# Applying a layer normalisation on ScalarE with scale and shift instead of on VectorE

## The chip, the core and the metric

The kernel runs on one core of a Trainium2 chip. The metric is the device time of one execution in microseconds, the median of three runs. Before the change it is 1572.69 us (1570.96 to 1573.69). The profile is of one further execution (1568.4 us, a traced span of 1566.6 us).

## What is computed

The input x has 32 graphs of 512 nodes with 128 features, and adj is a 512 by 512 adjacency. Layer 0 is a graph convolution with powers one to three of adj, layer 1 a gated graph network of five steps. Both add their input and normalise each node over its 128 features, with no learned gain:

```
m = mean(x);  v = var(x);  norm(x) = (x - m) / sqrt(v + 1e-5)
x = norm(x + conv(x, adj, weight_1))
h = x
five times:
    a  = adj @ h;  u3 = h @ u3_w.T + u3_b
    z  = sigmoid([a, a] @ w3_w.T + w3_b + u3)
    r  = sigmoid([a, a] @ w4_w.T + w4_b + u3)
    hv = tanh([a, a] @ w5_w.T + w5_b + (r * h) @ u5_w.T + u5_b)
    h  = (1 - z) * h + z * hv
out = norm(x + h)
```

## The kernel before

**Tiling.** The graphs are taken in 16 pairs (`pair(q)`, L584). Of each graph, 128 partitions hold nodes, with four groups of 128 features in the free dimension; the gates work on the transposed form (`hT`, features on partitions, 512 nodes). A product of adj by the state is made from seven block products instead of eight (`adj_product`, L349): sums S of blocks of the state are made on GpSimd (L372), TensorE multiplies them (L377), ScalarE copies partial sums out of PSUM into Q (L402, L412, L415), and VectorE adds (L404, L416, L422). Each next block product into the same PSUM bank waits for the copy of the one before it.

**One step of the gates** (`gates`, L545): TensorE multiplies by w4, w3, w5 and u5 (L550); VectorE adds biases (L555, L562), ScalarE applies sigmoids and tanh (L557, L564, L566, L576), VectorE makes `rh` (L558), GpSimd `rest` = (1 - z) * h (L569), and VectorE the new state hT (L578, L580). Then hT is brought back to nodes on partitions as X: for pairs below 15 by VectorE's 32 by 32 transposes (L333), a write to DRAM in four parts (L325) and a read back (L331); in pair 15 by TensorE (L251) and a copy (L632).

**The norms.** `norm` (L287) is used twice a pair and layer. In layer 0 it reads v, the copy of the convolution's result out of PSUM (L514), and writes `h0`; after the last step it reads and writes y, the sum of X and h0 (L643, GpSimd). For four groups of 128 features it takes moments on VectorE (L295, L296), then on GpSimd 1/sqrt(v + eps) for all four at once (`power`, L299 add and L300 power), then four applies on VectorE: (x - mean) * rstd (L303).

**The order.** Nothing is scheduled by hand. `Plan` (L41) records each operation with its engine, a planned duration, the operations that it follows, buffers that it takes and gives back, and a key. `run` (L69) plays a list schedule with these durations: each engine, when free, takes the ready operation with the smallest key. The instructions are written out in the order in which this play issues them, and each engine then works through its list in that order, whatever the real durations are. Keys grow by 33 from pair to pair and by 20 from step to step, so several pairs are in work at once, two at a time in the steps.

Of the kernel before, what the change touches and what calls it, by code (L numbers as in the profile page):

```python
# [9 lines left out]
F32 = mybir.dt.float32  # L10
AF = mybir.ActivationFunctionType
ALU = mybir.AluOpType
PSUM = bass.MemoryType.PSUM

P = 128
# [105 lines left out]
def gnn_resnorm_kernel(  # L121
# [17 lines left out]
    nc = tc.nc  # L139
# [147 lines left out]
    def norm(n, name, src_of, dst_of, after, give, key):  # L287

        mv = small.tile([P, n, 2], F32, tag="mv", name=f"mv_{name}")
        rstd = small.tile([P, n], F32, tag="rstd", name=f"rstd_{name}")  # L290
        got = []

        def moments(i):
            st = small.tile([P, 6], F32, tag="st", name=f"st_{name}_{i}")
            nc.vector.bn_stats(st, src_of(i))  # L295
            nc.vector.bn_aggr(mv[:, i, :], st)  # L296

        def power():
            nc.gpsimd.tensor_scalar(rstd, mv[:, :, 1], EPS, None, ALU.add)  # L299
            nc.gpsimd.tensor_tensor(rstd, rstd, mhalf[:, :n], ALU.pow)  # L300

        def apply(i):
            nc.vector.tensor_scalar(  # L303
                dst_of(i), src_of(i), mv[:, i, 0:1], rstd[:, i : i + 1], ALU.subtract, ALU.mult
            )

        for i in range(n):
            got.append(plan("DVE", 0.43, lambda i=i: moments(i), after=after, key=key))
        p = plan("POOL", 1.25, power, after=got, key=key)
        over = []  # L310
        for i in range(n):
            last = i == n - 1
            over.append(
                plan("DVE", 0.29, lambda i=i: apply(i), after=[p] + over, give=give if last else [], key=key)
            )
        return over

    def turn(src_of, dst_of, name, after, key, take=()):

        def put():
            for g in range(NR):
                nc.sync.dma_start(  # L325
                    plan[f"d{name}"][:, :, g, :].rearrange("r l f -> l r f"),
                    plan[f"v{name}"][g * R : (g + 1) * R, :].rearrange("l (r f) -> l r f", r=NR),
                )

        def fetch():  # L330
            nc.sync.dma_start(dst_of(), plan[f"d{name}"].rearrange("r l g f -> (r l) (g f)"))  # L331

        blocks = lambda: nc.vector.transpose(plan[f"v{name}"], src_of())  # L333
        t = plan("DVE", 0.75, blocks, after=after, take=[("v", f"v{name}")], key=key)
        t = plan("SP", 1.76, put, after=[t], take=[("d", f"d{name}")], give=[("v", f"v{name}")], key=key, late=1.8)
        return plan("SP", 0.35, fetch, after=[t], give=[("d", f"d{name}")], take=take, key=key, late=2.8)

# [11 lines left out]
    def adj_product(X_of, turned, name, m, after, key):  # L349
# [12 lines left out]
        def copied(i, block, after, take=()):  # L362

            on_act = i < 6
            to = nc.scalar.copy if on_act else nc.gpsimd.tensor_copy
            emit = lambda: to(fitted(i), block())  # L366
            engine, us = ("ACT", 0.4) if on_act else ("POOL", 0.75)
            return plan(engine, us, emit, after=after, take=take, key=key)

        def add(i, a, b, op):  # L370
# [13 lines left out]
                )  # L384

        def pool(i, a, b, op, after, take=()):
            return plan("POOL", 0.8, lambda: add(i, a, b, op), after=after, take=take, key=key)

        def pe(bank, left, right, first, last, after, take=(), give=()):
            emit = lambda: product(bank, left, right, first, last)  # L390
# [154 lines left out]
    def gates(q, s, b, name, m, h, h_new, after, u_done, key):  # L545

        mT, uT = m[1], f"uT{name}"
        pr, pz, ph = (f"b{g}{name}" for g in "rzh")
        rh, z, rest = (f"{g}{name}" for g in ("rh", "z", "rest"))
        mm = lambda dst, w, src, first, last: nc.tensor.matmul(  # L550
            plan[dst], lhsT=w, rhs=plan[src], start=first, stop=last
        )
        take = [("bank", pr), ("rh", rh), ("z", z), ("rest", rest), ("hT", h_new)]
        p = plan("PE", 0.86, lambda: mm(pr, w4s, mT, True, True), after=after + weights, take=take, key=key)
        emit = lambda: nc.vector.scalar_tensor_tensor(plan[pr], plan[pr], b4s, plan[uT], ALU.add, ALU.add)  # L555
        r = plan("DVE", 0.75, emit, after=[p, u_done], key=key)
        r = plan("ACT", 0.59, lambda: nc.scalar.activation(plan[pr], plan[pr], AF.Sigmoid), after=[r], key=key)  # L557
        emit = lambda: nc.vector.tensor_tensor(plan[rh], plan[pr], plan[h], ALU.mult)  # L558
        r = plan("DVE", 0.69, emit, after=[r], give=[("bank", pr)], key=key)

        p2 = plan("PE", 0.86, lambda: mm(pz, w3s, mT, True, True), after=[p], take=[("bank", pz)], key=key + 0.5)
        emit = lambda: nc.vector.scalar_tensor_tensor(plan[pz], plan[pz], b3s, plan[uT], ALU.add, ALU.add)  # L562
        t = plan("DVE", 0.75, emit, after=[p2, u_done], give=[("uT", uT)], key=key + 0.5)
        emit = lambda: nc.scalar.activation(plan[z], plan[pz], AF.Sigmoid)  # L564
        zs = plan("ACT", 0.59, emit, after=[t], key=key + 0.5)
        emit = lambda: nc.scalar.activation(plan[rest], plan[pz], AF.Sigmoid, scale=-1.0)  # L566
        t = plan("ACT", 0.59, emit, after=[t, zs], give=[("bank", pz)], key=key + 0.5)

        emit = lambda: nc.gpsimd.tensor_tensor(plan[rest], plan[rest], plan[h], ALU.mult)  # L569
        keep = plan("POOL", 1.3, emit, after=[t], key=key + 0.5)  # L570

        p3 = plan(
            "PE", 0.86, lambda: mm(ph, w5s, mT, True, False), after=[p2], take=[("bank", ph)], give=[m], key=key + 0.7
        )
        p4 = plan("PE", 0.86, lambda: mm(ph, u5s, rh, False, True), after=[p3, r], give=[("rh", rh)], key=key + 0.8)
        emit = lambda: nc.scalar.activation(plan[ph], plan[ph], AF.Tanh, bias=hv_b)  # L576
        t = plan("ACT", 0.66, emit, after=[p4], key=key + 0.8)
        emit = lambda: nc.vector.tensor_tensor(plan[ph], plan[ph], plan[z], ALU.mult)  # L578
        t = plan("DVE", 0.69, emit, after=[t, zs], give=[("z", z)], key=key + 0.8)
        emit = lambda: nc.vector.tensor_tensor(plan[h_new], plan[ph], plan[rest], ALU.add)  # L580
        give = [("bank", ph), ("rest", rest), ("hT", h)]
        return plan("DVE", 0.69, emit, after=[t, keep], give=give, key=key + 0.8)

    def pair(q):  # L584
# [6 lines left out]
        for s in range(STEPS):  # L591
# [25 lines left out]
            for b in range(2):  # L617
                nm = f"{name}_{b}"
                h_new = f"hT{nm}"
                g = gates(q, s, b, nm, m[b], h[b], h_new, got[b], u_done[b], key + 10)  # L620
                h[b] = h_new
                h_done.append([g])
                X_b = lambda b=b, name=name: plan[f"X{name}"][:, b]
                if q < TURNED:
                    h_of = lambda h_new=h_new: plan[h_new].rearrange("p (k r l) -> p r k l", r=NR, k=NK)
                    t = turn(h_of, X_b, nm, [g, x_slot], key + 15)
                else:
                    bn = f"bt{nm}"
                    emit = lambda bn=bn, h_new=h_new: transposes(plan[bn], lambda k: plan[h_new][:, chunk(k)])
                    t = plan("PE", 0.44, emit, after=[g, x_slot], take=[("bank", bn)], key=key + 15)  # L630

                    emit = lambda bn=bn, X_b=X_b: nc.scalar.copy(X_b(), plan[bn])  # L632
                    t = plan("ACT", 0.59, emit, after=[t], give=[("bank", bn)], key=key + 15)
                after.append([t])
                if not last:
                    continue

                i = 2 * q + b
                y = f"y{i}"

                def emit(b=b, y=y, X_new=X_new):
                    fit = lambda t: t.rearrange("p k (s d) -> p k s d", d=R) if q < TURNED else t
                    nc.gpsimd.tensor_tensor(fit(plan[y]), X_new(b), fit(plan[f"h0{q}"][:, b]), ALU.add)  # L643

                t = plan("POOL", 1.5, emit, after=[t], take=[("y", y)], key=key + 17)
                done.append(t)
                y_of = lambda k, y=y: plan[y][:, k, :]
                over = norm(NK, f"1_{i}", y_of, y_of, [t], [], key + 17)
                emit = lambda i=i, y=y: nc.sync.dma_start(out[i].rearrange("(p k) c -> p k c", k=NK), plan[y])
                plan("SP", 0.36, emit, after=over, give=[("y", y)], key=key + 17, late=2.0)  # L650
# [63 lines left out]
```

## Time and profile before

| | busy us | share of the span | instructions |
|---|---|---|---|
| TensorE (PE) | 1525.6 | 97% | 5944 |
| VectorE (DVE) | 990.3 | 63% | 2111 |
| ScalarE (ACT) | 703.9 | 45% | 1416 |
| GpSimd (POOL) | 610.7 | 39% | 770 |

| part of the norms | engine | count | mean ns |
|---|---|---|---|
| moments, L295 (layer 0 / last) | DVE | 128 / 128 | 270 / 267 |
| moments, L296 | DVE | 256 | 182 |
| add eps, L299 | POOL | 64 | 227 |
| power, L300 | POOL | 64 | 1036 |
| apply to h, L303 | DVE | 128 | 377 |
| apply to y, L303 | DVE | 128 | 582 |

Busy time is the time that an engine spends inside instructions. Moments of two kinds follow each other closely and overlap, so their lengths don't simply add. In a line of the timeline the columns are: start and length in us, engine, source line, operation, tiles written and read, and in brackets how long the engine had stood idle before it and what released it. TensorE is the busiest engine by far; the shares of the others say little before it is known in which places TensorE stands. The granted TensorE clock is 0.997 of full speed over the span.

### The profile page before, as it was taken

What the parts mean: (1) busy time and instruction counts of PE and PEld (TensorE: products, weight loads), DVE (VectorE), ACT (ScalarE), POOL (GpSimd) and SP (SyncE); (2) the same over time, 40 slices, a digit from 0 to 9 for tenths busy, and PEclk for the clock granted to TensorE, in tenths of its full rate; (3) what the DMA queues carried; (4) which work ended last, traced back from release to release, by engine and by line L of the source; (5) the groups of instructions that cost most, each with busy time, mean ns of one, the idle gap of its engine ahead of it and who ended that gap; (6) DMA issues with size and microseconds to landing.
All of it is one profiled execution on the core that took longest, in us unless ns stands there. A gap on an engine that the chain in (4) does not pass through costs nothing.

```text
span 1566.6 us, 19093 instructions
## 1 busy us (share of the span) xinstructions
PE 1525.6 (97%) x5944; PEld 1042.2 (67%) x5944; DVE 990.3 (63%) x2111; ACT 703.9 (45%) x1416; POOL 610.7 (39%) x770
## 2 busy tenths in 40 slices
PE   8999999999999999999999999999999999999995
PEld 6776676766767667676666766667676676766663
DVE  2455648576584765748666585765848657486756
ACT  2344435444353543535444444443535435356553
POOL 1233325334353352625334343343523526254434
PEclk9999999999999999999999999999999999999998
DMA  4021424224152421524323152231523223232211
GB/s 119 14 77 46 123 53 133 83 73 116 29 153 61 105 84 46 143 54 121 84 72 110 46 135 81 75 114 31 151 61 108 68 54 95 54 86 63 68 44 38
DMA packets 160181, 128.10 MB, mean 82 GB/s; under 512 B 18384, under 2 KB 124880, under 8 KB 160080
## 3 DMA queue, kind: packets, MB, share of 16 engines
q1 hardware_dynamic: 160080, 126.89, 29.9%
q8 instruction: 47, 0.77, 0.2%
q14 instruction: 54, 0.44, 0.1%
HBM read 64.42 MB, written 62.39 MB: 81 GB/s over the span
## 4 chain that ended last, share of the span: by engine, by line
PE 80%; DVE 8%; POOL 4%; DMA 2%; issue 2%; SPq 1%; ACT 1%; POOLq 0%; DVEq 0%; ACTq 0%
PE bank L550 30%; PE bank L377 28%; PE bank L598 7%; PE bank L488 7%; PE bank L499 4%; PE bank L458 3%; DVE y L303 3%; POOL y L643 2%; POOL rstd L300 1%; DMA X<-d 1%; DVE bank L555 1%; SPq L325 1%; POOL S L372 1%; PE bank L265 1%; DVE hT L580 1%
## 5 line engine op out<-in xcount | busy, mean ns | idle before, releaser
L569 POOL TENSOR_TENSOR rest<-rest,hT 128x512 f32<-128x512 f32 x160 | 203.0, 1270 | 704.5 <-ACT rest L566 704.2
L377 PE MATMUL bank<-T,S 128*128 128x256 f32 x1392 | 351.1, 380 | 1.6 <-ACT Q L412 1.5
L377 PEld LDWEIGHTS bank<-T,S 128*128 128x128 f32 x1392 | 263.0, 190 | 94.9 <-issue 25.3
L377 PE MATMUL bank<-at,S 128*128 128x256 f32 x864 | 222.1, 380 | 2.1 <-ACT S L366 1.2
L377 PEld LDWEIGHTS bank<-at,S 128*128 128x128 f32 x864 | 164.0, 190 | 51.2 <-issue 25.0
L578 DVE TENSOR_TENSOR bank<-bank,z 128x512 f32<-128x512 f32 x160 | 111.5, 697 | 120.7 <-ACT bank L576 120.6
L550 PE MATMUL bank<-m,w4s 128*128 128x512 f32 x320 | 155.7, 593 | 0.0
L550 PE MATMUL bank<-m,w3s 128*128 128x512 f32 x320 | 155.2, 593 | 0.0
L598 PE MATMUL bank<-hT,u3s 128*128 128x512 f32 x320 | 153.4, 593 | 0.0
L550 PE MATMUL bank<-rh,u5s 128*128 128x512 f32 x320 | 153.1, 593 | 0.3 <-DVE rh L558 0.3
L550 PE MATMUL bank<-m,w5s 128*128 128x512 f32 x320 | 152.7, 593 | 0.0
L372 POOL TENSOR_TENSOR S<-X 128x256 f32<-128x256 f32 x128 | 91.1, 727 | 142.3 <-DMA X<-d 141.3
L576 ACT ACTIVATE bank<-bank,hv_b 128x512 f32<-128x512 f32 x160 | 106.0, 662 | 75.2 <-PE bank L550 75.1
L557 ACT ACTIVATE bank<-bank 128x512 f32<-128x512 f32 x160 | 93.3, 583 | 99.6 <-DVE bank L555 97.2
L555 DVE SCALAR_TENSOR_TENSOR bank<-bank,b4s,uT 128x512 f32<-128x512 f32 x160 | 118.3, 746 | 30.0 <-PE bank L550 28.3
L603 ACT ACTIVATE uT<-bank,ub3s 128x512 f32<-128x512 f32 x160 | 108.8, 691 | 52.6 <-PE bank L598 50.5
L412 ACT COPY Q<-bank 128x256 f32<-128x256 f32 x96 | 36.0, 375 | 213.7 <-PE bank L377 213.6
L562 DVE SCALAR_TENSOR_TENSOR bank<-bank,b3s,uT 128x512 f32<-128x512 f32 x160 | 120.0, 751 | 2.8 <-PE bank L550 1.2
L488 PE MATMUL bank<-U,at 128*128 128x256 f32 x512 | 118.2, 380 | 0.0
L564 ACT ACTIVATE z<-bank 128x512 f32<-128x512 f32 x160 | 95.6, 597 | 43.3 <-DVE bank L562 41.7
L558 DVE TENSOR_TENSOR rh<-bank,hT 128x512 f32<-128x512 f32 x160 | 107.8, 681 | 10.3 <-ACT bank L557 10.0
L580 DVE TENSOR_TENSOR hT<-bank,rest 128x512 f32<-128x512 f32 x160 | 107.0, 676 | 4.6 <-POOL rest L569 0.2
(94 smaller groups left out, 2163.9 us busy)
## 6 DMA issues: line engine op xcount, KB each, us to landing
d<-v SPq DMA_DIRECT2D x824, 64.0 KB, 1.8
X<-d SPq DMA_DIRECT2D x150, 256.0 KB, 2.8
v<-d SPq DMA_DIRECT2D x56, 256.0 KB, 2.9
xg<-in_x SPq DMA_DIRECT2D x32, 256.0 KB, 2.9
out<-y SPq DMA_DIRECT2D x32, 256.0 KB, 2.0
at<-in_adjT SPq DMA_DIRECT2D x4, 256.0 KB, 5.3
X<-in_w SPq DMA_DIRECT2D x1, 448.0 KB, 6.2
rh<-in_w SPq DMA_DIRECT2D x3, 128.0 KB, 6.1
```

Source lines behind the costliest of these rows:

```text
L372: nc.gpsimd.tensor_tensor(fitted(i), a, b, op)
L377: nc.tensor.matmul(half(bank), lhsT=a[:, k, :], rhs=right[:, k, :], start=(first and k == 0), stop=(last and k == H - 1), skip_group_check ...
L488: nc.tensor.matmul(y_of()[:, j].rearrange("p b o -> p (b o)"), lhsT=at2[:, k, chunk(ko)], rhs=plan[f"U{q}"][:, k].rearrange("p b o -> p (b ...
L550: mm = lambda dst, w, src, first, last: nc.tensor.matmul(plan[dst], lhsT=w, rhs=plan[src], start=first, stop=last)
L555: emit = lambda: nc.vector.scalar_tensor_tensor(plan[pr], plan[pr], b4s, plan[uT], ALU.add, ALU.add)
L558: emit = lambda: nc.vector.tensor_tensor(plan[rh], plan[pr], plan[h], ALU.mult)
L562: emit = lambda: nc.vector.scalar_tensor_tensor(plan[pz], plan[pz], b3s, plan[uT], ALU.add, ALU.add)
L569: emit = lambda: nc.gpsimd.tensor_tensor(plan[rest], plan[rest], plan[h], ALU.mult)
L578: emit = lambda: nc.vector.tensor_tensor(plan[ph], plan[ph], plan[z], ALU.mult)
L580: emit = lambda: nc.vector.tensor_tensor(plan[h_new], plan[ph], plan[rest], ALU.add)
L598: emit = lambda bn=bn, hb=h[b]: nc.tensor.matmul(plan[bn], lhsT=u3s, rhs=plan[hb], start=True, stop=True)
L603: emit = lambda bn=bn, uT=uT: nc.scalar.activation(plan[uT], plan[bn], AF.Identity, bias=ub3s)
```

## The change

The apply becomes x * rstd + shift on ScalarE, with shift = -mean * rstd, which GpSimd makes in two more instructions for four groups at once. It is meant to take work off VectorE, whose queue holds the gates' additions. Beside that, planned durations are brought to what the trace shows; they only affect the order that the plan writes.

```diff
+        shift = small.tile([P, n], F32, tag="shift", name=f"shift_{name}")
...
         def power():
             nc.gpsimd.tensor_scalar(rstd, mv[:, :, 1], EPS, None, ALU.add)
+            nc.gpsimd.tensor_scalar(shift, mv[:, :, 0], -1.0, None, ALU.mult)
             nc.gpsimd.tensor_tensor(rstd, rstd, mhalf[:, :n], ALU.pow)
+            nc.gpsimd.tensor_tensor(shift, shift, rstd, ALU.mult)
 
         def apply(i):
-            nc.vector.tensor_scalar(
-                dst_of(i), src_of(i), mv[:, i, 0:1], rstd[:, i : i + 1], ALU.subtract, ALU.mult
+            nc.scalar.activation(
+                dst_of(i), src_of(i), AF.Identity, bias=shift[:, i : i + 1], scale=rstd[:, i : i + 1]
             )
 
         for i in range(n):
-            got.append(plan("DVE", 0.43, lambda i=i: moments(i), after=after, key=key))
-        p = plan("POOL", 1.25, power, after=got, key=key)
+            got.append(plan("DVE", 0.45, lambda i=i: moments(i), after=after, key=key))
+        p = plan("POOL", 1.75, power, after=got, key=key)
...
-                plan("DVE", 0.29, lambda i=i: apply(i), after=[p] + over, give=give if last else [], key=key)
+                plan("ACT", 0.3, lambda i=i: apply(i), after=[p] + over, give=give if last else [], key=key)
...
-        t = plan("DVE", 0.75, blocks, after=after, take=[("v", f"v{name}")], key=key)
+        t = plan("DVE", 0.7, blocks, after=after, take=[("v", f"v{name}")], key=key)
...
-            engine, us = ("ACT", 0.4) if on_act else ("POOL", 0.75)
+            engine, us = ("ACT", 0.41) if on_act else ("POOL", 0.4)
...
-            return plan("POOL", 0.8, lambda: add(i, a, b, op), after=after, take=take, key=key)
+            return plan("POOL", 0.73, lambda: add(i, a, b, op), after=after, take=take, key=key)
...
-        keep = plan("POOL", 1.3, emit, after=[t], key=key + 0.5)
+        keep = plan("POOL", 1.27, emit, after=[t], key=key + 0.5)
...
-                t = plan("POOL", 1.5, emit, after=[t], take=[("y", y)], key=key + 17)
+                t = plan("POOL", 1.27, emit, after=[t], take=[("y", y)], key=key + 17)
```

After the change all lines of the kernel below L303 stand three lines further down (the apply at L306, S sums at L375, Q copies at L405, L415 and L418, `rest` at L572).

## The prediction

> **What bounds the kernel now.** I read the busy table first, then the stretches of time, then what TensorE waited for.
>
> ```profile
> PE 1525.6 (97%) x5944; PEld 1042.2 (67%) x5944; DVE 990.3 (63%) x2111; ACT 703.9 (45%) x1416; POOL 610.7 (39%) x770
> ```
>
> TensorE is busy 1525.6 of 1566.6 us, and the change leaves its 5944 matmuls alone. So no edit can win more than the 41 us in which it stands. Where these lie, by stretch (the second number is TensorE's busy time):
>
> ```profile
> 0.00:40.00 40.00, 35.00 (x145) 24.80 (x146) 11.63 (x26) 8.91 (x17) 6.31 (x14) 1.00 0.40 117
> 1530.00:1540.00 10.00, 5.95 (x23) 3.05 (x22) 8.37 (x28) 5.00 (x9) 8.89 (x11) 1.00 0.07 26
> 1540.00:1550.00 10.00, 9.08 (x33) 5.77 (x32) 3.84 (x7) 2.49 (x6) 0.86 (x2) 1.00 0.07 26
> 1550.00:1567.00 17.00, 5.07 (x16) 2.27 (x14) 9.38 (x31) 4.58 (x8) 7.55 (x8) 0.67 0.08 31
> ```
>
> 5.0 us go to the first loads, 4.1 + 0.9 + 11.9 = 16.9 us to the end after 1530; about 19 us are left for the 1490 us between. TensorE's waits from 40 to 1530 us (total, times, longest) name them:
>
> ```profile
> PE bank L377 <- ACT Q L415: 15.8, 12, 1.9
> PE bank L377 <- ACT S L366: 1.2, 1, 1.2
> PE bank L377 <- ACT Q L412: 1.0, 2, 0.6
> ```
>
> Eleven of the twelve are one to a pair, from 240 to 1282 us (0.8 to 1.9 each). The timeline of one:
>
> ```profile
> 648.42 1.03 POOL L300 TENSOR_TENSOR rstd<-rstd,mhalf 128x4 f32<-128x4 f32 x1
> ...
> 649.06 3.91 DVE L303 TENSOR_SCALAR y<-y,mv,rstd 128x128 f32<-128x128 f32 x6
> ...
> 653.22 0.55 DVE L303 TENSOR_SCALAR y<-y,mv,rstd 128x128 f32<-128x128 f32 x1
> 653.69 1.40 DVE L555 SCALAR_TENSOR_TENSOR bank<-bank,b4s,uT 128x512 f32<-128x512 f32 x2
> ...
> 654.47 1.24 ACT L557 ACTIVATE bank<-bank 128x512 f32<-128x512 f32 x2 [1.74 <-DVE bank L555]
> ...
> 655.62 0.38 ACT L415 COPY Q<-bank 128x256 f32<-128x256 f32 x1
> ...
> 656.05 1.13 PE L377 MATMUL bank<-T,h 128*128 128x256 f32 x4 [1.14 <-ACT Q L415]
> ```
>
> VectorE spends 5.2 us on eight applies of the last normalisation (648.17 to 653.77), each between GpSimd's S sums; its L555 starts late; ScalarE, in order, stands in front of the sigmoid that needs L555; the copy L415 behind it comes late; TensorE stands 1.14 us. The cause is how long an apply takes (shortest, median, longest ns):
>
> ```profile
> L303 DVE TENSOR_SCALAR h<-v,mv,rstd x128: 304/340/883, 53.5 to 1377.3; 128x128 f32<-128x128 f32 x128
> L303 DVE TENSOR_SCALAR y<-y,mv,rstd x128: 297/743/883, 268.6 to 1563.2; 128x128 f32<-128x128 f32 x128
> ```
>
> The planner books 0.29 us for each. The layer-0 applies fit (0.34); the last ones take 0.74, about a GpSimd sum (0.727), so the written order is wrong just there.
>
> **What the Trainium skill says.** "SBUF — State Buffer", section "SBUF: two separate sides": VectorE and GpSimd share one port pair under an exclusive lock, and the loser "fully blocks"; ScalarE has its own ports. The trace agrees in size: 743 ns beside GpSimd against 297 alone. "VectorE: DVE Perf Modes", section "The perf-mode tier table", gives an fp32 tensor_scalar in SBUF the 2x mode, the one that needs both ports; this fits the 297 ns against 378 for a two-input 128x128 add. "ScalarE: Activation LUTs", section "Rules for kernel authors", prices an ACTIVATE with a bias pointer at about 0.3 us + 0.83 ns per element. The trace has no 128-wide one; its slope agrees ((585 - 373) ns / 256 = 0.83).
>
> **Part by part.**
>
> *Applies leave VectorE.* 256 instructions, 69.4 + 41.9 = 111.3 us, to about 879. Off the path but for the eleven places above, where eight applies booked at 2.3 us took 5.2; with them goes the cause of 15.3 us (15.8 less a last wait of 0.5 at 1470 to 1530, in the end's own stretch).
>
> *Applies come to ScalarE.* A 256-wide SBUF copy takes 410 ns; 128 elements less is -106; a bias adds 79 (tanh 662 against sigmoid 583) to 106 (L603 691 against 585). So 383 to 410 ns; the page's price gives 406. I take 400. Two L603 in a row took 1.28 us, so the second adds about 0.1 less than its length: a pitch of 0.3, which is what the plan now books. 256 x 0.4 = 102 us, ScalarE 806 us (51%). Identity is used by L603 and the trace has two table loads in all, so none is added.
>
> *Two more GpSimd instructions a norm.* A tensor_scalar of 128x4 takes 227 ns (L299). For the product, a line through 256 wide (727) and 512 wide (1270) gives 193 ns at four; I take 0.23, ends 0.19 and 0.73. With gaps as between L299 and L300 (0.08) a norm goes from 1.33 us (646.79 to 648.12) to about 1.9; planned 1.75. 64 x 0.46 = +29 us busy, GpSimd 641 us (41%). Queued behind it stand S sums (L375 after the change) and `rest` products (L572), for which TensorE and VectorE wait.
>
> *New wait on ScalarE.* The first apply waits for the shift; behind it in its queue stand copies Q, for which TensorE waits. I walked the changed program's written order at the same place, zero at the first matmul of `at` by `h`, one product or 512-wide matmul per 0.86 us. hT transposes stand earlier on VectorE, so X lands at about -5.7 and -3.8 instead of -2.2; both y sums end at -2.5, both `rest` products at 0.1, the first power at 2.0. The first S sum ends at 2.7, needed at 3.4. The second power runs 3.4 to 5.3, the next S sum ends at 6.0, needed at 6.0. ScalarE's applies end at 7.2, its copy Q is due at 7.1 and its successor product at 8.6. Nothing stands by much, but GpSimd has no slack: I leave 0.3 us a pair, 11 x 0.3 = 3.3, with 0 and 1.0 as ends. The layer-0 norm, walked likewise from 612 us, has its applies between L606 and the copies, done 0.1 us before a copy is due: 0.
>
> *Planned durations.* The changed numbers agree with the rows (0.40 for GpSimd's copy at 397 ns, 1.27 for L569, 0.73 for L372). They cost nothing; the order that follows from them is in the walks.
>
> *The end.* In pair 15 nothing fills TensorE. Now:
>
> ```profile
> 1527.33 0.68 DVE L558 TENSOR_TENSOR rh<-bank,hT 128x512 f32<-128x512 f32 x1
> ...
> 1529.48 1.26 POOL L643 TENSOR_TENSOR y<-X,h 128x512 f32<-128x512 f32 x1 [8.58 <-DMA X<-d]
> ...
> 1536.60 0.68 DVE L580 TENSOR_TENSOR hT<-bank,rest 128x512 f32<-128x512 f32 x1
> ```
>
> The changed order puts both moments of pair 14 (16 instructions, 3.1 us) ahead of both `rh`, and both powers ahead of both `rest` products. Counted from the gate's first matmul (1524.75): y ready at 2.1 to 4.7 (three products earlier than now, since pair 14's gates stand further ahead), moments end at 6.5, `rh` 7.9 (now 4.5), second power 8.8, `rest` on ScalarE between applies at 12.6, on GpSimd 14.3, second hT 15.1. Now it is 12.5 (1537.28). So +2.6. The final norm: power +0.6, four applies at a pitch of 0.3 and a last of 0.4 against 1.08: +0.2. Together +3.4.
>
> **Sum**: -15.3 + 3.3 + 3.4 = -8.6 us: 1572.7 - 8.6 = 1564.1.
>
> **The rivals.**
> - *All of it (0.15).* No stall is left, and y comes early enough that the end loses only the final norm: -15.3 + 0.8: 1558.2. For it: accurate durations. Against: the order of the end as written.
> - *GpSimd takes the stall over (0.11).* X lands 1 to 1.5 us later than I walked, and each microsecond goes through y, `rest`, power and S sum to TensorE: 11 x 1.0: -15.3 + 11 + 3.4 = -0.9: 1571.8. For it: GpSimd's longest waits are for transfers (X<-d 141 us). Against: VectorE frees hT earlier.
> - *ScalarE is blocked (0.12), slower.* An apply that waits for GpSimd holds a copy Q for about 0.9 us (half a power) in both norms of 15 pairs: 27 us, -15.3 + 27 + 3.4 = +15.1: 1587.8. For it: ScalarE's queue is in order and feeds TensorE three times a product. Against: in the trace it stands 5.6 us before L412 in just that place (5.61 at 652.36).
>
> **How the numbers follow.** The forecast (0.62) spans 1559 to 1568, since residual stalls of 0 to 0.7 a pair and an end of +0.8 to +5 both belong to it. 1556 to 1572 takes in the first two rivals and leaves out the slow one and the tails. Faster by 3.1 us or more (below 1569.5): 0.62 + 0.15 + a little of the second rival = 0.80; same 0.08; slower (above 1575.8) 0.12.
>
> **What would show it.** Right: the row PE L377 <- ACT Q (L418 after the change) falls from 15.8 to under 4 us; `rest` and hT of the last step come later from 1525 on, TensorE's idle after 1530 grows by about 3; applies near 400 ns, whichever buffer. Wrong: TensorE's waits name POOL S, or ScalarE's longest idle is an apply waiting for POOL shift with TensorE standing at once after; or applies of 0.6 us.

## The result, and the profile after

The changed kernel takes 1559.8 us (median of six runs, 1557.2 to 1562.6), the kernel before 1572.7 us in the same comparison (1569.2 to 1574.0). The ratio is 0.9922, with a 95% interval from 0.9906 to 0.9938. The forecast was 1564.1 us in a range of 1556 to 1572, so the direction and the range held, and the gain was 12.9 us instead of 8.6. The traced spans of the profiled executions are 1566.6 us before and 1555.4 us after; what follows explains these 11.2 us.

First the busy table of the changed kernel:

```profile
PE 1524.5 (98%) x5944; PEld 1041.3 (67%) x5944; DVE 894.2 (57%) x1855; ACT 801.9 (52%) x1672; POOL 635.8 (41%) x898
```

TensorE does the same work in the same busy time (1525.6 before). VectorE lost 96 us, ScalarE gained 98 and GpSimd 25. These shares are no explanation of the gain; what TensorE waited for is. From 40 to 1511 us (up to the gates of pair 15's fourth step) its waits are, in us in total, times and longest:

```profile
PE bank L380 <- POOL S L375: 2.9, 5, 1.2
PE bank L380 <- ACT Q L415: 2.4, 2, 1.9
PE bank L380 <- ACT Q L418: 0.9, 2, 0.5
```

From 240 to 1300 us only the first of these rows is left. The kernel before has this row there and no other:

```profile
PE bank L377 <- ACT Q L415: 15.3, 11, 1.9
```

The place that the prediction showed at 648 us now reads as follows (timeline after: start, length, engine, line, operation, tiles; in brackets the idle time before and what ended it):

```profile
638.78 0.23 POOL L300 TENSOR_SCALAR rstd<-mv 128x4 f32<-128x4 f32 x1
639.10 0.23 POOL L301 TENSOR_SCALAR shift<-mv 128x4 f32<-128x4 f32 x1
639.29 1.04 POOL L302 TENSOR_TENSOR rstd<-rstd,mhalf 128x4 f32<-128x4 f32 x1
...
640.40 0.20 POOL L303 TENSOR_TENSOR shift<-shift,rstd 128x4 f32<-128x4 f32 x1
...
640.55 1.42 POOL L375 TENSOR_TENSOR S<-h 128x256 f32<-128x256 f32 x2
...
640.64 1.65 ACT L306 ACTIVATE y<-y,shift,rstd 128x128 f32<-128x128 f32 x4 [0.32 <-POOL shift L303]
...
641.42 1.05 PE L380 MATMUL bank<-T,S 128*128 128x256 f32 x4
```

GpSimd needs 1.82 us for one norm (638.78 to 640.60). The four applies follow on ScalarE in 1.65 us, a pitch of 0.39, beside two S sums that no longer hold them back. No bracket stands behind the TensorE line: it did not wait.

The idle time in a row of waits understates what a stall costs. It counts from the recorded end of the matmul before, and a matmul of 256 columns is recorded with 0.38 us where the next usually starts after 0.22; that hides 0.16 us of each stall. And after each of the stalls from 240 to 1300 us the second matmul started 0.32 us behind the first instead of 0.22. So I measured the loss from start to start: each matmul's start, less the start of the one before and the usual distance of such a pair. For pair 15, where nothing fills TensorE, I took whole stretches: E is the first matmul by w4 of its fourth step, F that of its fifth.

| us | before | after | difference |
|---|---|---|---|
| lost, 40 to 240 | 3.96 | 2.49 | -1.5 |
| lost, 240 to 1300 | 18.66 | 4.67 | -14.0 |
| from E to F | 21.53 | 24.96 | +3.4 |
| from F to the end | 20.3 | 21.4 | +1.1 |
| sum | | | -11.0 |

The four rows give 11.0 of the 11.2 us by which the spans differ.

### The profile page after: what moved, and what is told of

The parts are those of the page before. It is cut to its first block, busy times and chain, and to the rows that moved or that the text cites. A ratio compares the mean times of both kernels' runs of the same rounds, so it can differ in the third digit from the quotient of the medians.

```text
span 1555.4 us, 19232 instructions
## 1 busy us (share of the span) xinstructions
PE 1524.5 (98%) x5944; PEld 1041.3 (67%) x5944; DVE 894.2 (57%) x1855; ACT 801.9 (52%) x1672; POOL 635.8 (41%) x898
## 4 chain that ended last, share of the span: by engine, by line
PE 92%; POOL 2%; issue 2%; DMA 1%; DVE 1%; ACT 1%; SPq 0%; ACTq 0%; POOLq 0%; DVEq 0%
PE bank L380 35%; PE bank L553 33%; PE bank L601 8%; PE bank L491 7%; PE bank L461 4%; PE bank L502 4%; PE bank L265 1%; DMA X<-d 1%; POOL rest L572 1%; PE bank L251 1%; POOL S L375 1%; POOL rstd L302 0%; POOL y L646 0%; SPq L328 0%; DMA at<-in_adjT 0%
## 5 line engine op out<-in xcount | busy, mean ns | idle before, releaser
L572 POOL TENSOR_TENSOR rest<-rest,hT 128x512 f32<-128x512 f32 x160 | 202.7, 1270 | 590.7 <-ACT rest L569 586.5
L375 POOL TENSOR_TENSOR S<-X 128x256 f32<-128x256 f32 x128 | 91.1, 726 | 150.0 <-DMA X<-d 132.5
L553 PEld LDWEIGHTS bank<-rh,u5s 128*128 128x128 f32 x320 | 60.7, 190 | 70.8 <-issue 58.8
```

Source lines behind the costliest of these rows:

```text
L375: nc.gpsimd.tensor_tensor(fitted(i), a, b, op)
L553: mm = lambda dst, w, src, first, last: nc.tensor.matmul(plan[dst], lhsT=w, rhs=plan[src], start=first, stop=last)
```

## The end of the changed kernel

The end gave back 4.5 us. The timeline after, around the fourth step of pair 15 (E is at 1509.05):

```profile
1514.81 1.25 DVE L561 TENSOR_TENSOR rh<-bank,hT 128x512 f32<-128x512 f32 x2
...
1515.53 1.98 PE L553 MATMUL bank<-rh,u5s 128*128 128x512 f32 x4 [1.17 <-DVE rh L561]
...
1520.16 2.49 POOL L572 TENSOR_TENSOR rest<-rest,hT 128x512 f32<-128x512 f32 x2 [3.02 <-ACT rest L569]
...
1522.20 1.11 PE L251 MATMUL bank<-ident,hT 128*128 128x128 f32 x4 [4.69 <-DVE hT L583]
1522.86 0.69 DVE L583 TENSOR_TENSOR hT<-bank,rest 128x512 f32<-128x512 f32 x1
...
1523.11 1.91 PE L601 MATMUL bank<-hT,u3s 128*128 128x512 f32 x2
...
1524.82 0.91 PE L251 MATMUL bank<-ident,hT 128*128 128x128 f32 x4
```

Both `rh` are made at E+5.8 to E+7.0, behind the sixteen moments of pair 14; before, the second ended at E+4.5. Both `rest` products are done at E+13.6. The second hT ends at 1523.55, which is E+14.5 against E+12.5 before: 2.0 us from the order. The rest is of another kind. TensorE had stood 4.69 us; the windows of the same stretch show what it then ran at (length; busy time of PE, PEld, DVE, ACT, POOL; granted clock; DMA share; GB/s):

```profile
1518.00:1522.00 4.00, 0.00 (x0) 0.00 (x0) 1.24 (x2) 3.49 (x8) 1.84 (x2) 1.00 0.28 109
1522.00:1525.00 3.00, 2.80 (x7) 1.66 (x8) 1.45 (x3) 0.59 (x1) 1.37 (x2) 0.50 0.02 8
```

At a granted clock of 0.50 the four transposes took 1.11 us and the two matmuls by u3s 1.91 us. In the kernel before, where TensorE had stood 2.13 us, it was 0.66 and 1.02 us:

```profile
1533.91 0.66 PE L251 MATMUL bank<-ident,hT 128*128 128x128 f32 x4 [2.13 <-DVE hT L580]
1534.40 1.02 PE L598 MATMUL bank<-hT,u3s 128*128 128x512 f32 x2
...
1537.34 0.66 PE L251 MATMUL bank<-ident,hT 128*128 128x128 f32 x4 [1.91 <-DVE hT L580]
```

So the second transposes start 1.3 us after their hT (1523.55 to 1524.82) instead of 0.06 us (1537.28 to 1537.34). From E they are 3.2 us later than before: 2.0 by order, 1.2 by the clock.

## The experiments

Two theories stood at the start. **The engine**: the gain comes from taking the applies off VectorE, where GpSimd's sums hold them back. **The plan**: it comes from planned durations that agree with the chip, so that the order as written is right. The rival of both was that ScalarE, blocked by an apply, holds the copies for TensorE. Each number of time below is a median with its ratio to the kernel before on the same chip (1570.6 to 1572.8 us). Not all experiments ran on one chip, so the ratios are what to compare.

**Durations alone.** Only the planned numbers of the change, on the kernel before; the apply stays on VectorE, planned at 0.29.

```diff
-            got.append(plan("DVE", 0.43, lambda i=i: moments(i), after=after, key=key))
+            got.append(plan("DVE", 0.45, lambda i=i: moments(i), after=after, key=key))
...
-            engine, us = ("ACT", 0.4) if on_act else ("POOL", 0.75)
+            engine, us = ("ACT", 0.41) if on_act else ("POOL", 0.4)
...
-            return plan("POOL", 0.8, lambda: add(i, a, b, op), after=after, take=take, key=key)
+            return plan("POOL", 0.73, lambda: add(i, a, b, op), after=after, take=take, key=key)
...
-                t = plan("POOL", 1.5, emit, after=[t], take=[("y", y)], key=key + 17)
+                t = plan("POOL", 1.27, emit, after=[t], take=[("y", y)], key=key + 17)
```

> The kernel before with the changed planned durations alone (moments 0.45, transposes 0.7, GpSimd copy 0.4, S sums 0.73, rest 1.27, y sum 1.27); the applies stay on VectorE, booked at 0.29, and the power at 1.25. My theory (the gain is the eleven stalls behind the slow applies of the last norm): the applies still take 0.74 us where 0.29 is booked, so about one stall of L377 behind a Q copy stays in each pair: 1571 to 1574, within 0.2% of before. Rival (the order written from better durations is the gain): 1561 to 1564.

Measured: 1565.7 us, 0.9953 (0.9940 to 0.9965). A part of the gain comes without any work moved to another engine. The loss from 240 to 1300 us falls from 18.7 to 13.3; the wait is the old one, only shorter:

```profile
PE bank L377 <- ACT Q L415: 6.9, 11, 0.7
```

**Operations alone.** The changed kernel with all old durations: apply on ScalarE at 0.29, power at 1.25, and the others (not shown) as before.

```diff
-        p = plan("POOL", 1.75, power, after=got, key=key)
+        p = plan("POOL", 1.25, power, after=got, key=key)
...
-                plan("ACT", 0.3, lambda i=i: apply(i), after=[p] + over, give=give if last else [], key=key)
+                plan("ACT", 0.29, lambda i=i: apply(i), after=[p] + over, give=give if last else [], key=key)
```

> The changed kernel with the old planned durations (the apply at 0.29 on ScalarE, the power of four instructions at 1.25). My theory: the applies are off VectorE, so most of the 15 us is kept; the plan is wrong by 0.6 us on each power, which is given back in small waits of TensorE for GpSimd's S sums: 1558 to 1565. Rival (the durations are the gain): 1570 or more.

Measured: 1571.6 us, 0.9993 (0.9984 to 1.0002), no gain, where the theory of the engine expected most of it. TensorE's waits of this kernel from 240 to 1300 us name another copy than before:

```profile
PE bank L380 <- ACT Q L405: 6.0, 11, 0.6
PE bank L380 <- POOL S L375: 3.5, 6, 1.1
PE bank L380 <- ACT Q L415: 0.3, 1, 0.3
```

And its timeline shows the chain in the layer-0 norm:

```profile
614.45 0.20 POOL L303 TENSOR_TENSOR shift<-shift,rstd 128x4 f32<-128x4 f32 x1
...
614.68 1.26 ACT L306 ACTIVATE h<-v,shift,rstd 128x128 f32<-128x128 f32 x3 [0.72 <-POOL shift L303]
...
615.85 0.35 ACT L405 COPY Q<-bank 128x256 f32<-128x256 f32 x1
...
616.35 1.10 PE L380 MATMUL bank<-T,S 128*128 128x256 f32 x4 [0.55 <-ACT Q L405]
```

ScalarE stands 0.72 us for a shift, three applies follow, then the copy for which TensorE stands 0.55. This is the rival "ScalarE is blocked". It needs only that the planner believes the shift to come 0.6 us earlier than it does (1.25 planned, 1.83 taken: 612.82 to 614.65). The old wait has all but gone with the applies (L415, 0.3 us); another has come in its place. Not run was this kernel with the power at 1.75 and all else old, so whether the move by itself gains once its own power is planned right stays open.

**Each norm alone on ScalarE**, with the new durations: first the last norm only, then the layer-0 norm only.

```diff
+        on_act = name.startswith("1_")
...
-        p = plan("POOL", 1.75, power, after=got, key=key)
+        p = plan("POOL", 1.75 if on_act else 1.25, power, after=got, key=key)
...
+                plan(*(("ACT", 0.3) if on_act else ("DVE", 0.29)), lambda i=i: apply(i), after=[p] + over, give=give if last else [], key=key)
```

> The changed kernel with only the last norm on ScalarE; the layer-0 applies go back to VectorE at 0.29 and their power to two instructions at 1.25. My theory: the stalls sat behind the last norm's applies only, so the whole gain stays: 1557 to 1562, and TensorE's waits between 240 and 1282 us stay under 5 us. Rival (ScalarE's relief of VectorE by 42 us in layer 0 counts as well): 1564 to 1568.

> The changed kernel with only the layer-0 norm on ScalarE; the last norm's applies stay on VectorE, booked at 0.29. My theory: the stalls stay, 1570 to 1575. Rival (any 42 us less on VectorE help by their share): 1564 to 1568.

 (The edit is the same with "0_" in place of "1_".)

Measured: last norm alone 1560.3 us, 0.9926 (0.9914 to 0.9939), as much as the whole change. Layer-0 norm alone 1562.9 us, 0.9942 (0.9929 to 0.9956), well below what was expected of it. Here the applies to y stay on VectorE, planned at 0.29 as before, and yet the loss from 240 to 1300 falls to 11.3 us. Most of that belongs to the durations, which alone gave 13.3 and 0.9953 (0.9940 to 0.9965); the two intervals overlap, so a worth of the layer-0 norm's move is not shown.

**The apply left on VectorE, but planned as long as it takes.** The durations of the first experiment, and the apply to y at 0.7.

```diff
-        p = plan("POOL", 1.25, power, after=got, key=key)
+        p = plan("POOL", 1.33, power, after=got, key=key)
...
-                plan("DVE", 0.29, lambda i=i: apply(i), after=[p] + over, give=give if last else [], key=key)
+                plan("DVE", 0.7 if name.startswith("1_") else 0.34, lambda i=i: apply(i), after=[p] + over, give=give if last else [], key=key)
```

> The kernel before with all the better durations and the applies left on VectorE, but booked at what they take: 0.7 in the last norm, 0.34 in layer 0, the power at 1.33. Theory now (what counts is that the plan's durations agree with the chip's in the stretch of the last norm, on whichever engine the applies are): TensorE's time lost between 240 and 1300 us falls from 13.3 (durations alone, applies booked at 0.29) to under 8, total 1560 to 1564. Rival (VectorE is really held by the applies beside GpSimd's sums, so that only moving them helps): 12 us or more lost there, total 1565 to 1570.

Measured: 1553.8 us, 0.9895 (0.9880 to 0.9911), much better than expected and at least as good as the change itself (the intervals overlap by 0.0005). The applies are as slow as ever (shortest, median, longest ns, VectorE's line of this kernel):

```profile
L303 DVE TENSOR_SCALAR y<-y,mv,rstd x128: 298/743/886, 266.1 to 1548.0; 128x128 f32<-128x128 f32 x128
```

But TensorE's waits from 240 to 1300 us are down to one row,

```profile
PE bank L377 <- POOL S L372: 0.4, 1, 0.4
```

and the timeline shows why the slow applies hurt nobody:

```profile
639.35 1.02 PE L550 MATMUL bank<-m,w4s 128*128 128x512 f32 x2
...
640.56 4.04 DVE L303 TENSOR_SCALAR y<-y,mv,rstd 128x128 f32<-128x128 f32 x6
...
641.07 1.02 PE L550 MATMUL bank<-m,w4s 128*128 128x512 f32 x2
641.27 0.37 ACT L412 COPY Q<-bank 128x256 f32<-128x256 f32 x1 [3.88 <-PE bank L377]
...
642.99 0.37 ACT L415 COPY Q<-bank 128x256 f32<-128x256 f32 x1 [1.35 <-PE bank L377]
...
643.66 1.03 PE L377 MATMUL bank<-T,h 128*128 128x256 f32 x4
```

The six applies take 4.04 us. Since the planner knows that L555 comes late behind them, it writes the copies L412 and L415 ahead of the sigmoid L557 that needs L555. In the brackets the copies now wait for TensorE, and TensorE for nothing.

**One wrong number put back into the changed kernel**: the power at 1.25, the rest as changed.

```diff
-        p = plan("POOL", 1.75, power, after=got, key=key)
+        p = plan("POOL", 1.25, power, after=got, key=key)
```

> The changed kernel with one number put back: the power of four instructions booked at 1.25 instead of 1.75. Theory (in the kernel with the old durations the applies on ScalarE stood in front of a copy Q because the power was booked 0.6 us short): the wait of L380 behind L405 comes back, about 0.7 us in each of eleven pairs, and total 1564 to 1570. Rival (another of the old durations did that): 1558 to 1562 as in the changed kernel.

Measured: 1573.4 us, 1.0017 (1.0009 to 1.0025): more lost than expected, the whole gain and a little beyond. The waits are those of "operations alone":

```profile
PE bank L380 <- ACT Q L405: 5.9, 11, 0.5
PE bank L380 <- POOL S L375: 3.6, 10, 0.4
```

**One right number put into an otherwise old order.** The durations of the first experiment with nothing but 0.7 for the apply to y added; then the kernel before with nothing but that.

```diff
-                plan("DVE", 0.29, lambda i=i: apply(i), after=[p] + over, give=give if last else [], key=key)
+                plan("DVE", 0.7 if name.startswith("1_") else 0.29, lambda i=i: apply(i), after=[p] + over, give=give if last else [], key=key)
```

> The better durations alone (as in the first run of this study) with one more number: the last norm's applies booked at 0.7 instead of 0.29; layer 0's applies stay at 0.29 and the power at 1.25. Theory (the apply's booking is the number that misled the plan): time lost between 240 and 1300 us falls from 13.3 to under 4, total 1553 to 1557. Rival (the power's 0.08 or layer 0's 0.05 count too): 6 us or more lost, total 1558 to 1562.

> The kernel before with one number changed: the last norm's applies booked at 0.7 instead of 0.29, all other durations old (S sums at 0.8, GpSimd copies 0.75, y sums 1.5). Theory (the apply's number alone is the main error): 1556 to 1562. Rival (the numbers have to be right together, as moving the applies with the old durations gave nothing): 1566 or more.

Measured: 1557.9 us, 0.9912 (0.9896 to 0.9928), 0.9 us above the range of the theory and with 3.0 us lost within it, and 1558.5 us, 0.9915 (0.9901 to 0.9928). The second is the kernel before, line for line, with one planned duration corrected. From 240 to 1300 us its TensorE waits this much:

```profile
PE bank L377 <- POOL S L372: 0.5, 1, 0.5
```

Its interval overlaps that of the whole change over most of its length. So the gain needs no other engine, only this number in the plan. That 0.7 helps because it agrees with the chip, and not because any larger number would write the copies earlier, rests on the place followed above and on the loss that came back with the power's wrong number; no third value was tried for the apply.

The first of the two differs from the well-planned VectorE version only by the power (1.25 for 1.33) and the layer-0 apply (0.29 for 0.34). From 40 to 240 us it loses 3.3 us and that one 0.1. The rival that these small numbers count is right there.

**The end.** Pair 14's last norm gets a later key, so that pair 15's gates go first; in a second kernel two of the four applies of the last pair's last norm go to VectorE beside.

```diff
-                over = norm(NK, f"1_{i}", y_of, y_of, [t], [], key + 17)
+                over = norm(NK, f"1_{i}", y_of, y_of, [t], [], key + (60 if q == NP - 2 else 17))
```

> The changed kernel with the key of pair 14's last norm 43 higher, so that pair 15's rh, rest and tanh stand before its moments, powers and applies; nothing before the end moves. Theory (the end lost 3.4 us to that order: VectorE's hT of the last step 2 us later, and 1.3 us because TensorE ran slowly after standing 4.7 us): the stretch from pair 15's fourth gates to the end shrinks from 46.4 to 42.5 to 43.5 us, the transposes of hT take about 0.66 again, total 1556 to 1558. Rival (the end is longer only for the longer power and the slower applies): under 1 us.

> The same, and in pair 15's last norm groups 2 and 3 of each graph are applied on VectorE, which stands idle then. The last four applies take 1.65 us in the changed kernel; two take 0.87: 0.8 us less than the kernel without it, total 1555 to 1557.

Measured: 1553.4 us, 0.9891 (0.9878 to 0.9905), better than expected, and 1553.7 us, 0.9892 (0.9877 to 0.9907). With the later key E to F takes 20.1 us instead of 25.0, less than in the kernel before. TensorE stands 1.61 us ahead of the first transposes and not 4.69, and these then run at full clock:

```profile
1519.19 0.66 PE L251 MATMUL bank<-ident,hT 128*128 128x128 f32 x4 [1.61 <-DVE hT L583]
...
1519.68 1.02 PE L601 MATMUL bank<-hT,u3s 128*128 128x512 f32 x2
```

Splitting the last applies shortens F to the end by 0.5 us in the trace (21.4 to 20.9) instead of the 0.8 expected, which the times don't resolve.

**Both together**: the well-planned VectorE version with the later key, and the changed kernel with the later key and the apply planned at 0.42.

```diff
-                plan("ACT", 0.3, lambda i=i: apply(i), after=[p] + over, give=give if last else [], key=key)
+                plan("ACT", 0.42, lambda i=i: apply(i), after=[p] + over, give=give if last else [], key=key)
```

> The kernel with the applies on VectorE and booked at what they take, with pair 14's last norm put off to the end as well (key 43 higher). Theory (two separate gains: 17 us of lost time between 240 and 1300 us by agreeing durations, about 4 us at the end by the order there): 1548 to 1551. Rival (the applies on VectorE stand in the way of the last step's additions, which ScalarE's did not): 1552 to 1556.

> The changed kernel with pair 14's last norm put off and the applies on ScalarE booked at 0.42, between the pitch of 0.39 in a row and the 0.48 of one alone. Theory (agreement, on either engine): 4 to 6 us lost between 240 and 1300 us fall to 1 to 3, total 1550 to 1552. Rival (what is left are waits for GpSimd's S sums behind the longer power, which this number does not touch): 1553 to 1554 as without it.

Measured: 1551.2 us, 0.9864 (0.9850 to 0.9878) on VectorE, just above the range expected, and 1551.5 us, 0.9870 (0.9855 to 0.9885) on ScalarE. Both beat the two kernels of the change, and they can't be told apart. With the order right on both sides, the engine of the apply is worth nothing that can be measured here.

The losses of all runs side by side, in us from their traces:

| kernel | 40 to 240 | 240 to 1300 | E to F | F to end | ratio |
|---|---|---|---|---|---|
| before | 4.0 | 18.7 | 21.5 | 20.3 | 1 |
| after | 2.5 | 4.7 | 25.0 | 21.4 | 0.9922 |
| durations alone | 3.5 | 13.3 | 24.6 | 20.4 | 0.9953 |
| operations alone | 2.4 | 15.5 | 27.0 | 21.6 | 0.9993 |
| last norm on ScalarE | 3.6 | 6.7 | 25.9 | 21.6 | 0.9926 |
| layer-0 norm on ScalarE | 1.9 | 11.3 | 23.5 | 20.1 | 0.9942 |
| VectorE, well planned | 0.1 | 1.5 | 24.5 | 21.0 | 0.9895 |
| after, power at 1.25 | 3.4 | 15.9 | 26.2 | 21.4 | 1.0017 |
| after, later key | 1.8 | 5.8 | 20.1 | 21.4 | 0.9891 |
| after, later key, split | 2.4 | 3.6 | 20.1 | 20.9 | 0.9892 |
| VectorE, well planned, later key | 0.1 | 3.6 | 20.2 | 21.0 | 0.9864 |
| durations and one number | 3.3 | 3.0 | 24.9 | 21.1 | 0.9912 |
| after, 0.42, later key | 0.7 | 3.4 | 20.2 | 21.4 | 0.9870 |
| before and one number | 4.1 | 0.8 | 24.6 | 21.0 | 0.9915 |

Two things go with this table. The rows don't add up to the differences of the spans, for two stretches are left out. In the first 40 us, with the first loads, the runs lose 3.5 to 6.4 us. From 1300 us to E the kernel before and the changed one lose 2.4 and 2.2 us, but "before and one number" loses 4.4, and the two well-planned VectorE kernels, "durations and one number", "after, 0.42, later key" and "after, power at 1.25" lose 3.8 to 3.9. And each row is one trace. The two well-planned VectorE kernels have the same instructions in the same order on every engine up to pair 14's last norm, and still lose 1.5 and 3.6 us from 240 to 1300. Three more, the changed kernel and the two with the later key, also share one order up to there and lose 4.7, 5.8 and 3.6. Differences of about 2 us in this column show nothing.

The longer way from E to F is no matter of the engine either: it is 24.6 us in two kernels whose applies never left VectorE (durations alone, before and one number).

## Why the prediction was right, and where its sizes were off

**The place of the gain: right.** It put -15.3 + 3.3 = -12.0 us on the stalls in pairs below 15. Measured from start to start it is -14.0 in 240 to 1300. The term was mis-sized by its unit: 15.3 us of idle time were 18.7 us lost, since each of the eleven stalls cost 0.27 us beyond its recorded idle time (0.16 for the overlap of two matmuls that it ends, 0.10 for the slower start) and a twelfth of 0.12 us idle stands in no row. The residue was planned as 11 x 0.3 = 3.3 us; it came as five waits for POOL S, 2.9 us idle and 4.7 lost. "TensorE's waits name POOL S" was given as a sign of being wrong and came true, but at 2.9 us and not at the 11 of its rival. Another 1.5 us came from 40 to 240, where nothing was forecast.

**The walk: right within 0.6 us.** Counted from the first matmul of `at` by h (637.96), the first power ends at 2.6 (walked 2.0), the first S sum at 3.3 (2.7), the second power at 5.9 (5.3), the next sum at 6.6 (6.0). All is later by the same 0.6, as both y sums end at -1.7 instead of -2.5, and TensorE still doesn't stand here. GpSimd had more slack than "no slack" said: the product that needs the second sum starts at 6.9 (644.88, with six of the gate's matmuls ahead of it), not at 6.0.

**The end: right in kind, 1.1 us too small.** Forecast +3.4. The order's part was 2.6 and is 2.0; every step of the walk came 0.6 to 0.9 us early (second `rh` E+7.0 for 7.9, second hT E+14.5 for 15.1). The term that was missing is the clock after a stall of 4.7 us: +1.2. The final norm was +0.8 and is +1.1: the power +0.5 (0.6 forecast), the applies +0.5 (0.2 forecast).

**The apply's price: too low.** The forecast took 400 ns and a pitch of 0.3. The two rows of the changed line:

```profile
L306 ACT ACTIVATE h<-v,shift,rstd x128: 477/487/503, 53.9 to 1361.9; 128x128 f32<-128x128 f32 x128
L306 ACT ACTIVATE y<-y,shift,rstd x128: 472/480/507, 267.2 to 1551.8; 128x128 f32<-128x128 f32 x128
```

480 ns, a pitch of 0.39. The sum had a term for the bias (79 to 106 ns) and none for the scale, which this form also reads per partition. The 80 ns missing are of that size; no run separates the two. ScalarE's busy time still grew as forecast (+98 for +102), because applies in a row overlap. VectorE's fell by 96 us and not by 111, which lies off the path. "Whichever buffer" held: h and y take the same, beside GpSimd or not. The figure of 406 ns worked out from the Trainium skill's page "ScalarE: Activation LUTs" (section "Rules for kernel authors") counts a bias read per partition and no such scale; measured are 480 ns. GpSimd's additions came close, 1.82 us a norm for 1.9:

```profile
L301 POOL TENSOR_SCALAR shift<-mv 128x4 f32<-128x4 f32 x64 | 14.5, 226 | 5.1
L303 POOL TENSOR_TENSOR shift<-shift,rstd 128x4 f32<-128x4 f32 x64 | 12.9, 202 | 5.0
```

**Two readings.** The eight applies at 648 us filled 4.7 us of VectorE's time within a stretch of 5.6, not 5.2, and two of them stood beside no S sum. And 297 ns against 378 for a two-input 128x128 add shows no mode of VectorE: that add (L217) reads one input with a step of seven elements, and the three that read both inputs without a step take 282 to 285 ns:

```profile
L231 DVE TENSOR_TENSOR w3s<-rh 128x128 f32<-128x128 f32 x1 | 0.3, 285 | 0.0
```

**The cause: one step too deep.** "The cause is how long an apply takes" was the step that failed. "Applies leave VectorE ... with them goes the cause" is half right: the old wait goes with them, but the time comes back only if the plan's numbers fit what replaces it. Applies of 743 ns cost nothing where they are planned at 0.7; applies of 480 ns on ScalarE gained nothing under the old durations. The cause is the distance between planned and real, 0.29 against 0.74, and the sentence after it ("so the written order is wrong just there") had it. That the forecast was near all the same is because the change closes this distance too, by giving the applies to an engine where its number 0.3 agrees with the pitch of 0.39 well enough.

**The slow rival.** "ScalarE is blocked" didn't occur in the changed kernel, and it isn't a matter of 12 in 100 but of a single number: with the power planned at 1.25 it is there. It cost 0.5 to 0.6 us of idle time each and not the 0.9 that the rival assumed, in eleven places and not in both norms of fifteen pairs; the one followed above is a layer-0 norm.

**Left open.** Which of the small corrections in "durations alone" brought its 7 us was not separated. Nor is it known what lets one and the same order lose 2 us more in one run than in another. The medians differ by 12.9 us and the profiled spans by 11.2, because the profiled executions are single ones (1568.4 and 1557.2 us) that lie 4.3 and 2.6 us below their medians.

## What to carry to other kernels

Where a list schedule writes the order from planned durations, compare every planned number with the trace before moving any work to another engine, and take the duration from the place in question: one operation can take 340 ns in one stage and 743 in another. One number that is off by half a microsecond, at a place on the feeding engine's queue, was worth as much here as the whole change, in both directions. At the end of a kernel, where nothing fills TensorE, put finishing work of the pair before behind the last pair's chain.

## What the runs showed of the hardware

- What slows a VectorE apply is a GpSimd sum, not GpSimd as such. In the trace of before the apply takes 340 ns (median of 96) with nothing beside it, 336 ns (45) beside the 128x4 power alone, though that takes 1.04 us, and 761 ns (89) beside an S sum; 88 of these 89 end 81 to 86 ns after a sum ends. The forecast had only "about a GpSimd sum". The Trainium skill's page "SBUF — State Buffer", section "SBUF: two separate sides", speaks of an exclusive lock on the port pair, held for the whole instruction, that blocks the other engine; that fits the sums and isn't seen with the power.
- A TensorE that had stood 4.7 us was granted half its clock for 3.4 us around its next start, which alone made 1.2 us here. Of the fourteen kernels, nine stood 4.3 to 5.7 us in the fourth step of pair 15, and all nine were granted half the clock then, for 3.4 us in two of them and 6.8 in seven; the five that stood at most 2.1 us there kept the full clock. With the later key it had stood 1.6 us at the same place, and its transposes ran at 0.66 us, that is at full clock. A short stop is no safe bound, though: in the last step of the kernel before, two stops of 1.43 and 0.75 us were followed by transposes of 1.11 us, and in the changed kernel the same two stops by 0.66.
- A stall between matmuls of 256 columns cost TensorE 0.27 us more than the idle time that the waits show: 0.16 because the recorded length of a matmul (0.38) exceeds its usual distance to the next (0.22), and 0.10 because the second matmul after the stall started 0.32 us behind the first.
